# Feed-forward input transposed by VectorE and by way of DRAM in a fused attention and feed-forward kernel

## The chip, the cores and the metric

The kernel runs on one core of one Trainium2 chip. The time is device time of one execution in microseconds (us); lower is better. Everything is float32. Engines are named as in the profile: PE is TensorE, PEld its weight loads, DVE is VectorE, ACT is ScalarE, POOL is GpSimd, SP is SyncE, which here only issues DMAs.

## What is computed

One layer on 2048 tokens of width 256: a differential attention with 16 query and 8 key heads, then a gated feed-forward with Walsh-Hadamard transforms. Both are wrapped the same way: normalise, apply, normalise, add.

```python
x = x + _layernorm(_L0_attn_ref(_layernorm(x), ...))
x = x + _layernorm(_L0_ffn_ref(_layernorm(x), ...))

def _L0_ffn_ref(input, SU_ug, SU_dp, Wscale_ug, Wscale_dp, W_up, W_gate, W_down):
    x = fwht(x * SU_ug) / SCALE
    x_up = x @ W_up.T * (Wscale_ug[:INTER] * SCALE)
    x_gate = x @ W_gate.T * (Wscale_ug[INTER:] * SCALE)
    x = jax.nn.silu(x_gate) * x_up
    x = fwht(x * SU_dp) / SCALE
    return x @ W_down.T * (Wscale_dp * SCALE)
```

HIDDEN is 256 and INTER is 1024. The transforms are linear and are folded into the weights on the chip beforehand, so that per token the feed-forward is two products (gate and up, 256 to 1024), an elementwise step and one product (down, 1024 to 256).

## The kernel before

**Attention** is cut into 96 units of query rows, 24 for each of 4 groups of heads. Each unit goes through stages one step apart: `scores` on PE, the running minimum on DVE (L276, L287), `exponentials` on ACT, `combine` on DVE, then `turn`, which transposes 32x32 blocks on DVE (L353) and writes them to DRAM, `arrive`, which reads them back turned, `values` on PE (L377), `inverse` on POOL, `turn_out` and `arrive_out` (the same way by DRAM for the output, L421, L423, L433), `project_out` on PE (L442) and `accumulate` on DVE into `acc`, which holds the attention output of all tokens.

**Feed-forward** goes over blocks b of 256 tokens from b = 7 down to 0 (NS is 8), since the last group of heads finishes the late rows first. Partition p of a block holds two tokens, t = 0 and 1. The functions of a block:

- `load_x(b)`: POOL issues two DMAs of the residual x into `xr` (two buffers).
- `front1(b)`: statistics of the attention output (DVE, then a power on POOL, L93).
- `front2(b)`: normalises it (L97), adds x (L641), statistics of the sum.
- `front3(b)`: normalises the sum into `xr` (L97).
- `turn_ffn(b)`: four PE transposes of 128x128 into PSUM (`tx`, L653), one ACT copy into `fxnT` (L655), which holds features on partitions and the 256 tokens in columns, t = 0 in the first 128.
- `hidden(b, k)`, k = 0 to 3: 16 matmuls for gate and up (L666) into one PSUM tile; for each of its two chunks of 128 hidden features a sigmoid on ACT (L679) and two products on DVE (L680, L681) into `hT` (ten buffers).
- `back(b)`: 32 matmuls (L696) of `hT` with the down weights into `pd`.
- `finish1(b)`, `finish2(b)`: statistics of `pd`, normalisation, the sum with `acc`, and two DMAs of the result (L715).

PSUM tiles of the scores, of the hidden pieces, of `tx` and of `pd` share three buffers of one tag (`sc`). The two DVE transposes of `turn_out` write into one buffer (`xo`), which is free again when its DMA to DRAM (a tile of tag `do`, four buffers) has landed.

**Order.** The order of every engine's instructions is the order of the calls. The generator `ffn_pieces` yields the feed-forward in pieces. The list at the end of the kernel places the pieces into the attention's steps: block 7's hidden pieces in the last four steps with new units, then two pieces per step (before the step's own work and between), and all that is left after the last step. `last` is the number of units; `put(before, last - 5, turn_ffn, NS - 1)` places a call ahead of the work of step `last - 5`. Block 7's `load_x` and `front1` to `front3` stand near step `last - 11`. For the others the generator sets the order: after hidden(b, 0) come `front2(b-1)` and back(b+1), then finish(b+1) and hidden(b, 1), then `front3(b-1)` and hidden(b, 2), then `turn_ffn(b-1)`, `front1(b-2)` and hidden(b, 3), then hidden(b-1, 0).

Of the kernel before, what the change touches and what calls it, by code (L numbers as in the profile page):

```python
# [10 lines left out]
F32 = mybir.dt.float32  # L11
# [5 lines left out]
P = 128  # L17
# [11 lines left out]
NS = S // 256  # L29
# [19 lines left out]
def kernel(  # L49
# [14 lines left out]
    nc = tc.nc  # L64
# [3 lines left out]
    ident = const.tile([P, P], F32, name="ident")  # L68
# [14 lines left out]
    def rstd_of(pool, src, n, tag):  # L83

        st = pool.tile([P, 4, 6], F32, tag="st" + tag, name="st" + tag)
        mv = pool.tile([P, 4, 2], F32, tag="mv" + tag, name="mv" + tag)
        for t in range(n):
            nc.vector.bn_stats(st[:, t, :], src[t] if isinstance(src, list) else src[:, t, :])
            nc.vector.bn_aggr(mv[:, t, :], st[:, t, :])
        ve = pool.tile([P, 4], F32, tag="ve" + tag, name="ve" + tag)  # L90
        nc.vector.tensor_scalar(ve[:, :n], mv[:, :n, 1], EPS, None, ALU.add)
        rstd = pool.tile([P, 4], F32, tag="rs" + tag, name="rs" + tag)
        nc.gpsimd.tensor_tensor(rstd[:, :n], ve[:, :n], mhalf[:, :n], ALU.pow)  # L93
        return mv, rstd

    def normalise(dst, src, mv, rstd, t):
        nc.vector.tensor_scalar(  # L97
            dst, src, mv[:, t, 0:1], rstd[:, t : t + 1], ALU.subtract, ALU.mult
        )
# [7 lines left out]
    with ExitStack() as actx:  # L107
        ep = actx.enter_context(tc.tile_pool(name="ep", bufs=3))
        op = actx.enter_context(tc.tile_pool(name="op", bufs=2))
# [3 lines left out]
        dram = actx.enter_context(tc.tile_pool(name="dram", bufs=4, space=bass.MemoryType.DRAM))  # L113
        ps_s = actx.enter_context(tc.tile_pool(name="ps_s", bufs=3, space=PSUM))
# [11 lines left out]
        xnT = xtp.tile([P, 2, S], F32, name="xnT")  # L126
# [418 lines left out]
        ffn = {}  # L545
# [82 lines left out]
        def load_x(b):  # L628
            ffn["xr", b] = ffn["p"].tile([P, 2, HID], F32, tag="xr", name=f"xr_{b}", bufs=2)
            for s in range(2):  # L630
                nc.gpsimd.dma_start(ffn["xr", b][s::2], x2[b, s])


        def front1(b):
            ffn["ln", b] = rstd_of(ffn["p"], acc[:, ts(b, 2), :], 2, "a")

        def front2(b):
            y = acc[:, ts(b, 2), :]
            for t in range(2):
                normalise(y[:, t, :], y[:, t, :], *ffn["ln", b], t)  # L640
            nc.vector.tensor_add(y, ffn["xr", b], y)  # L641
            ffn["ln", b] = rstd_of(ffn["p"], y, 2, "b")

        def front3(b):
            for t in range(2):
                normalise(ffn["xr", b][:, t, :], acc[:, 2 * b + t, :], *ffn["ln", b], t)

        def turn_ffn(b):
            xr = ffn["xr", b]
            tx = ps_s.tile([P, 1024], F32, tag="sc", name=f"tx_{b}")[:, :512]  # L650
            for c in range(2):
                for t in range(2):
                    nc.tensor.transpose(tx[:, ts(2 * c + t, P)], xr[:, t, ts(c, P)], ident)  # L653
            xnT = ffn["p"].tile([P, 2, 256], F32, tag="fxnT", name=f"fxnT_{b}", bufs=2)
            nc.scalar.copy(xnT.rearrange("p c q -> p (c q)"), tx)  # L655
            ffn["xnT", b] = xnT

        def hidden(b, k):

            ps = ps_s.tile([P, 1024], F32, tag="sc", name=f"gu_{b}_{k}")  # L660
            xnT = ffn["xnT", b]
            for j in range(2):
                fc = 2 * k + j
                for n, which in enumerate(("gate", "up")):
                    for c in range(2):
                        nc.tensor.matmul(  # L666
                            ps[:, ts(2 * j + n, 256)],
                            lhsT=ffn[which][:, c, ts(fc, P)],
                            rhs=xnT[:, c, :],
                            start=(c == 0),  # L670
                            stop=(c == 1),
                        )
            for j in range(2):
                fc = 2 * k + j
                pg, pu = ps[:, ts(2 * j, 256)], ps[:, ts(2 * j + 1, 256)]
                wsu = colv[:, C_WSUG + fc : C_WSUG + fc + 1]
                wsg = colv[:, C_WSUG + NFC + fc : C_WSUG + NFC + fc + 1]
                hT = ffn["p"].tile([P, 256], F32, tag="hT", name=f"hT_{b}_{fc}", bufs=10)
                nc.scalar.activation(hT, pg, AF.Sigmoid, scale=wsg)  # L679
                nc.vector.scalar_tensor_tensor(hT, pg, wsg, hT, ALU.mult, ALU.mult)  # L680
                nc.vector.scalar_tensor_tensor(hT, pu, wsu, hT, ALU.mult, ALU.mult)  # L681
                ffn["hT", b, fc] = hT

        def back(b):

            if b:
                pd = ps_s.tile([P, 2, 512], F32, tag="sc", name=f"pd_{b}")
                pd = [pd[:, t, :HID] for t in range(2)]
            else:
                pd = [  # L690
                    ps_s.tile([P, 1024], F32, tag="sc", name=f"pd_{b}_{t}")[:, :HID]
                    for t in range(2)
                ]
            for t in range(2):
                for fc in range(NFC):
                    nc.tensor.matmul(  # L696
                        pd[t],
                        lhsT=ffn["hT", b, fc][:, ts(t, P)],
                        rhs=ffn["down"][:, fc, :],
                        start=(fc == 0),  # L700
                        stop=(fc == NFC - 1),
                    )
            ffn["pd", b] = pd

        def finish1(b, lo=0, n=2):
            ffn["ln", b, lo] = rstd_of(ffn["p"], ffn["pd", b][lo : lo + n], n, "c")

        def finish2(b, lo=0, n=2):
            tag, bufs = ("xr", 2) if lo else ("y", 1)
            z = ffn["p"].tile([P, 2, HID], F32, tag=tag, name=f"y_{b}_{lo}", bufs=bufs)[:, :n, :]  # L710
            for t in range(n):
                normalise(z[:, t, :], ffn["pd", b][lo + t], *ffn["ln", b, lo], t)
            nc.vector.tensor_add(z, z, acc[:, 2 * b + lo : 2 * b + lo + n, :])
            for s, engine in enumerate((nc.sync, nc.sync if b else nc.scalar)):
                engine.dma_start(outv[b, s][:, lo : lo + n, :], z[s::2])  # L715

        def ffn_pieces():
            for b in range(NS - 1, -1, -1):
                prev, nxt = b + 1 < NS, b > 0
                if nxt:  # L720
                    load_x(b - 1)
                yield hidden(b, 0)
                if nxt:
                    front2(b - 1)
                if prev:
                    yield back(b + 1)
                    finish1(b + 1)
                    finish2(b + 1)
                yield hidden(b, 1)
                if nxt:  # L730
                    front3(b - 1)
                yield hidden(b, 2)
                if nxt:
                    turn_ffn(b - 1)
                    if b > 1:
                        front1(b - 2)
                yield hidden(b, 3)
            back(0)
            for lo in range(2):
                finish1(0, lo, 1)  # L740
                finish2(0, lo, 1)

        pieces = ffn_pieces()

        def ffn_piece():
# [12 lines left out]
        before, mid, between, after = {}, {}, {}, {}  # L758

        def put(where, step, f, *args, **kw):  # L760
            where.setdefault(step, []).append(lambda: f(*args, **kw))
# [63 lines left out]
        last = len(units)  # L825
# [20 lines left out]
        begun = first + 13  # L846
        put(after, begun, open_ffn)
        put(after, begun, load_x, NS - 1)
        for j, part in enumerate((front1, front2, front3)):
            put(after, begun + j, part, NS - 1)  # L850
        put(after, begun + 2, front1, NS - 2)
        put(before, last - 5, turn_ffn, NS - 1)
        for where, step, count in (
            *((between, last - 4 + j, 1) for j in range(4)),
            *((w, last + j, 1) for j in range(LAG + 3) for w in (before, between)),
# [98 lines left out]
```

## Time and profile before

| | us |
|---|---|
| median of 3 runs (1462.11 to 1464.83) | 1464.06 |
| the profiled execution | 1462.91 |
| span of the profiled execution | 1461.1 |
| L653, PE transposes of `xr`, 32 instructions, busy | 5.9 |
| L655, ACT copies of `tx`, 8 instructions, busy | 4.6 |
| L666, PE matmuls of the hidden pieces, 512 instructions, busy | 131.5 |
| L696, PE matmuls of back, 256 instructions, busy | 56.8 |
| L421, DVE transposes of `turn_out`, 128 instructions, busy | 48.9 |

The granted clock of TensorE is 0.999 over the span. Busy time by stage:

```profile
1200.00:1250.00 50.00, 48.65 (x198) 37.09 (x197) 39.59 (x112) 23.96 (x59) 7.96 (x21) 1.00 0.89 185
1250.00:1300.00 50.00, 49.29 (x231) 42.90 (x231) 34.20 (x117) 27.68 (x69) 13.16 (x28) 1.00 0.39 102
...
1380.00:1400.00 20.00, 20.00 (x95) 17.66 (x95) 13.59 (x36) 3.98 (x9) 3.29 (x5) 1.00 0.06 19
```

The columns are the stretch and its length, then busy time with the number of instructions for PE, PEld, DVE, ACT and POOL, the granted clock, the share of DMA time and GB/s. Block 7's feed-forward begins at 1236 us; the last attention matmul (L442) ends near 1351 us; from there to the end only feed-forward blocks run. In a group of pipelined matmuls the length shown for one is longer than the distance to the next; the distance between the starts of two groups is what a group costs. A bracket behind an instruction holds the idle time ahead of it and the engine and line that ended it.

### The profile page before, as it was taken

Reading aid. Unit: us, or ns where it says so; the run is one execution under the profiler, and the core shown is the slowest. Engines: PE = TensorE matmul, PEld = TensorE weight load, DVE = VectorE, ACT = ScalarE, POOL = GpSimd, SP = SyncE. Lnnn points to the kernel's source line nnn. Section 1 sums busy time; section 2 is a strip of 40 time slices with the busy share of each in tenths; the row PEclk is TensorE's granted clock in tenths of the full one; section 3 lists DMA queues with packets and bytes.
Section 4 is the critical chain, followed back from the end, with each engine's and each line's share of the span. In section 5 each row is a group of like instructions: output and inputs, shape, how many; then the busy total and the mean of one; then the engine's idle time right before and its main releaser. Section 6 shows DMA issues by size and latency. Waiting matters only on the chain.

```text
span 1461.1 us, 17617 instructions
## 1 busy us (share of the span) xinstructions
PE 1441.2 (99%) x5484; PEld 1040.1 (71%) x5484; DVE 1038.5 (71%) x2412; ACT 516.9 (35%) x1125; POOL 359.1 (25%) x683
## 2 busy tenths in 40 slices
PE   8999999999999999999999999999999999999998
PEld 7567767756766777675677776675777767888887
DVE  5588888847666889644968779536877898756674
ACT  2453333323133334333333344333333444631211
POOL 2026735542007851011111111111111111121110
PEclk9999999999999999999999999999999999999999
DMA  3169889856487888831798888621999998522000
GB/s 116 33 162 195 185 194 220 167 103 132 91 194 147 164 190 198 170 80 51 155 184 177 172 202 169 141 65 52 194 209 189 196 183 181 131 79 58 30 22 15
DMA packets 494828, 204.50 MB, mean 140 GB/s; under 512 B 391088, under 2 KB 491952, under 8 KB 494736
## 3 DMA queue, kind: packets, MB, share of 16 engines
q1 hardware_dynamic: 491120, 194.17, 63.3%
q0 software_dynamic: 2480, 8.26, 2.1%
q8 instruction: 45, 0.74, 0.2%
q10 hardware_dynamic: 1136, 0.95, 0.2%
q14 instruction: 47, 0.39, 0.1%
HBM read 107.90 MB, written 95.42 MB: 139 GB/s over the span
## 4 chain that ended last, share of the span: by engine, by line
PE 92%; DVE 6%; issue 1%; ACT 1%; DMA 1%; SPq 0%; POOL 0%; POOLq 0%; DVEq 0%; ACTq 0%
PE po L377 30%; PE sc L261 29%; PE pp L173 11%; PE pout L442 7%; PE gu L666 7%; PE pv L202 4%; PE pd L696 4%; DVE e L276 1%; DVE e L334 1%; DVE e L353 1%; DMA wq<-in_wqkvT 1%; DVE e L287 0%; PE tx L653 0%; DVE xo L421 0%; DVE cf L329 0%
## 5 line engine op out<-in xcount | busy, mean ns | idle before, releaser
L261 PE MATMUL sc<-k,q 128*128 128x512 f32 (+7 forms) x1280 | 478.6, 520 | 8.7 <-DVE last L287 3.7
L377 PE MATMUL po<-v,pt 128*128 128x256 f32 x2176 | 485.4, 379 | 0.0
L377 PEld LDWEIGHTS po<-v,pt 128*128 128x128 f32 x2176 | 425.9, 196 | 57.1 <-issue 9.5
L261 PEld LDWEIGHTS sc<-k,q 128*128 128x128 f32 x1280 | 236.7, 190 | 229.3 <-issue 184.3
L302 ACT ACTIVATE e<-e,last 128x192 f32<-128x192 f32 (+28 forms) x256 | 299.6, 1171 | 217.9 <-DVE last L287 205.3
L276 DVE TENSOR_SCALAR_CACHE_REDUCE e<-sc 128x1024 f32<-128x1024 f32 (+15 forms) x248 | 231.1, 932 | 188.6 <-PE sc L261 187.8
L402 POOL TENSOR_TENSOR u<-ss,ed 128x1 f32<-128x1 f32 (+1 forms) x96 | 18.3, 191 | 764.7 <-ACT po L391 764.5
L388 ACT COPY osb<-po 128x256 f32<-128x256 f32 (+1 forms) x96 | 42.5, 443 | 457.5 <-PE po L377 450.1
L353 DVE STREAM_TRANSPOSE e<-e 128x768 f32<-128x768 f32 (+7 forms) x192 | 172.3, 937 | 6.7
L334 DVE SCALAR_TENSOR_TENSOR e<-e,cf,e 128x64 f32<-128x64 f32 (+31 forms) x128 | 173.8, 1378 | 3.4
L173 PE MATMUL pp<-xnT,wq 128*128 128x512 f32 (+1 forms) x408 | 170.8, 568 | 2.8 <-DMA wq<-in_wqkvT 2.6
L173 PEld LDWEIGHTS pp<-xnT,wq 128*128 128x128 f32 x408 | 76.7, 190 | 81.1 <-issue 74.6
L442 PE MATMUL pout<-wo,oT 128*128 128x256 f32 x512 | 120.9, 379 | 0.0
L276 DVE TENSOR_SCALAR_CACHE_REDUCE e<-sc,mx 128x320 f32<-128x320 f32 (+13 forms) x128 | 97.1, 759 | 21.3 <-PE sc L261 7.8
L442 PEld LDWEIGHTS pout<-wo,oT 128*128 128x128 f32 x512 | 97.3, 190 | 12.8
L679 ACT ACTIVATE hT<-gu,colv 128x256 f32<-128x256 f32 x64 | 30.3, 473 | 132.6 <-PE gu L666 91.1
L287 DVE CUSTOM_DVE_ANT_0 e<-sc,mask,mx 128x64 f32<-128x64 f32 x248 | 70.4, 284 | 8.9
L666 PE MATMUL gu<-fxnT,wgate 128*128 128x256 f32 x256 | 65.8, 379 | 0.2 <-DVE last L287 0.2
L666 PE MATMUL gu<-fxnT,wup 128*128 128x256 f32 x256 | 65.7, 379 | 0.0
L405 POOL TENSOR_SCALAR osb<-osb,f 128x256 f32<-128x256 f32 x128 | 61.3, 479 | 12.3
L403 POOL TENSOR_TENSOR f<-u,mhalf 128x1 f32<-128x1 f32 (+1 forms) x96 | 60.0, 625 | 7.5
L680 DVE SCALAR_TENSOR_TENSOR hT<-gu,colv,hT 128x256 f32<-128x256 f32 x64 | 30.9, 482 | 41.7 <-ACT hT L679 41.5
(102 smaller groups left out, 1112.6 us busy)
## 6 DMA issues: line engine op xcount, KB each, us to landing
dr<-e SPq DMA_DIRECT2D x20, 1024.0 KB, 4.7
pt<-dr SPq DMA_DIRECT2D x80, 256.0 KB, 5.9
dr<-e SPq DMA_DIRECT2D x20, 896.0 KB, 4.4
pt<-dr SPq DMA_DIRECT2D x80, 224.0 KB, 5.1
do<-xo SPq DMA_DIRECT2D x64, 256.0 KB, 3.8
oT<-do SPq DMA_DIRECT2D x256, 64.0 KB, 2.6
dr<-e SPq DMA_DIRECT2D x20, 768.0 KB, 4.3
pt<-dr SPq DMA_DIRECT2D x80, 192.0 KB, 4.4
```

The source lines that it names most:

```text
L173: nc.tensor.matmul(pp[:, 512 * h : 512 * h + n], lhsT=wq[:, c, ts(j, P)], rhs=xnT[:, c, cols4], start=(c == 0), stop=(c == 1),)
L261: nc.tensor.matmul(sc[:, 512 * k : 512 * k + ww], lhsT=qT[m][:, u.i, u.subs[a]].rearrange("d p q -> d (p q)"), rhs=kT[m][:, at + lo : at + ...
L276: nc.vector.tensor_scalar(dst, src, 1.0, best, ALU.mult, ALU.min, accum_out=u.mx[:, k0, c : c + 1],)
L287: nc.vector.tensor_tensor_reduce(e[:, L - 64 : L], sc[:, tail : tail + 64], mask, 1.0, best, ALU.add, ALU.min, accum_out=u.last[:, k0 : k0 ...
L302: nc.scalar.activation(e, e, AF.Exp, bias=u.last[:, 2 * a + m : 2 * a + m + 1], scale=-1.0, accum_out=u.d[:, a, m : m + 1],)
L334: nc.vector.scalar_tensor_tensor(e0, e1, cf[:, a : a + 1], e0, ALU.mult, ALU.add)
L353: nc.vector.transpose(xv[:, r], ev[:, r])
L377: nc.tensor.matmul(u.po[:, ts(a, HID)], lhsT=ptv[:, g, r, :], rhs=vt[:, kc, :], start=(kc == 0), stop=(kc == u.i),)
L403: nc.gpsimd.tensor_tensor(f[:, : u.ns], w[:, : u.ns], mhalf[:, : u.ns], ALU.pow)
L405: nc.gpsimd.tensor_scalar(u.osb[:, a, :], u.osb[:, a, :], f[:, a : a + 1], 16.0, ALU.mult, ALU.mult)
L442: nc.tensor.matmul(u.pout[:, :HID], lhsT=u.oT[:, c, p, :], rhs=wos[u.g][:, p, c, :], start=(p == 0 and c == 0), stop=(p == 1 and c == 1),)
L666: nc.tensor.matmul(ps[:, ts(2 * j + n, 256)], lhsT=ffn[which][:, c, ts(fc, P)], rhs=xnT[:, c, :], start=(c == 0), stop=(c == 1),)
```

## The change

The four PE transposes, the PSUM tile `tx` and the ACT copy are taken out. `turn_ffn` now does what `turn_out` does: two DVE transposes of 32x32 blocks into the shared buffer `xo`, and one DMA on SP to a DRAM tile of the tag `do`. A new function `arrive_ffn` reads the block back with four DMAs on SP, one for each 32 partitions of `fxnT`, in rows of 64 elements. Token columns of `fxnT` now alternate between t = 0 and t = 1, so `back` reads its weights from `hT` with a step of two. In the generator `front3(b-1)`, `turn_ffn(b-1)` and `arrive_ffn(b-1)` stand right behind back(b+1) and ahead of finish(b+1), and `front1(b-2)` stays ahead of hidden(b, 3). Block 6 is taken out of the generator and is loaded, normalised and turned by calls placed in the attention's steps, as block 7 is; block 7's turn moves from step `last - 5` to `last - 7`, its reads to `last - 6`.

```diff
--- before.py
+++ after.py
@@ -646,13 +646,26 @@
                 normalise(ffn["xr", b][:, t, :], acc[:, 2 * b + t, :], *ffn["ln", b], t)
 
         def turn_ffn(b):
-            xr = ffn["xr", b]
-            tx = ps_s.tile([P, 1024], F32, tag="sc", name=f"tx_{b}")[:, :512]
-            for c in range(2):
-                for t in range(2):
-                    nc.tensor.transpose(tx[:, ts(2 * c + t, P)], xr[:, t, ts(c, P)], ident)
+
+            xo = op.tile([P, 512], F32, tag="xo", name=f"xf_{b}", bufs=1)
+            xv = xo.rearrange("p (g a c r) -> p r g a c", a=4, g=2, r=2)
+            ev = ffn["xr", b].rearrange("p r (g a c) -> p r g a c", g=2, a=4)
+            for r in range(2):
+                nc.vector.transpose(xv[:, r], ev[:, r])
+            dr = dram.tile([2, 4, 32, 4, 64], F32, tag="do", name=f"df_{b}")
+            nc.sync.dma_start(
+                dr.rearrange("g b q a w -> (b q) g (a w)"),
+                xo.rearrange("p (g w) -> p g w", g=2),
+            )
+            ffn["dx", b] = dr
+
+        def arrive_ffn(b):
             xnT = ffn["p"].tile([P, 2, 256], F32, tag="fxnT", name=f"fxnT_{b}", bufs=2)
-            nc.scalar.copy(xnT.rearrange("p c q -> p (c q)"), tx)
+            for a in range(4):
+                nc.sync.dma_start(
+                    xnT[ts(a, 32)].rearrange("e c (b w) -> e (c b) w", w=64),
+                    ffn["dx", b][:, :, :, a, :].rearrange("g b q w -> q (g b) w"),
+                )
             ffn["xnT", b] = xnT
 
         def hidden(b, k):
@@ -695,7 +708,7 @@
                 for fc in range(NFC):
                     nc.tensor.matmul(
                         pd[t],
-                        lhsT=ffn["hT", b, fc][:, ts(t, P)],
+                        lhsT=ffn["hT", b, fc][:, t::2],
                         rhs=ffn["down"][:, fc, :],
                         start=(fc == 0),
                         stop=(fc == NFC - 1),
@@ -717,23 +730,24 @@
         def ffn_pieces():
             for b in range(NS - 1, -1, -1):
                 prev, nxt = b + 1 < NS, b > 0
-                if nxt:
+                if nxt and prev:
                     load_x(b - 1)
                 yield hidden(b, 0)
-                if nxt:
+                if nxt and prev:
                     front2(b - 1)
                 if prev:
                     yield back(b + 1)
+                if nxt and prev:
+                    front3(b - 1)
+                    turn_ffn(b - 1)
+                    arrive_ffn(b - 1)
+                if prev:
                     finish1(b + 1)
                     finish2(b + 1)
                 yield hidden(b, 1)
-                if nxt:
-                    front3(b - 1)
                 yield hidden(b, 2)
-                if nxt:
-                    turn_ffn(b - 1)
-                    if b > 1:
-                        front1(b - 2)
+                if b > 1:
+                    front1(b - 2)
                 yield hidden(b, 3)
             back(0)
             for lo in range(2):
@@ -848,8 +862,14 @@
         put(after, begun, load_x, NS - 1)
         for j, part in enumerate((front1, front2, front3)):
             put(after, begun + j, part, NS - 1)
+        put(after, begun + 2, load_x, NS - 2)
         put(after, begun + 2, front1, NS - 2)
-        put(before, last - 5, turn_ffn, NS - 1)
+        put(before, last - 7, turn_ffn, NS - 1)
+        put(before, last - 6, arrive_ffn, NS - 1)
+        put(after, last - 5, front2, NS - 2)
+        put(after, last - 4, front3, NS - 2)
+        put(before, last - 3, turn_ffn, NS - 2)
+        put(before, last - 2, arrive_ffn, NS - 2)
         for where, step, count in (
             *((between, last - 4 + j, 1) for j in range(4)),
             *((w, last + j, 1) for j in range(LAG + 3) for w in (before, between)),
```

## The prediction

> **What bounds the kernel now.** I read the busy totals first, then the chain of waits, then tables by stage of the last 260 us, where the feed-forward blocks run, and last the order of time on TensorE, VectorE and the DMA queue there.
>
> ```profile
> PE 1441.2 (99%) x5484; PEld 1040.1 (71%) x5484; DVE 1038.5 (71%) x2412; ACT 516.9 (35%) x1125; POOL 359.1 (25%) x683
> ...
> PE 92%; DVE 6%; issue 1%; ACT 1%; DMA 1%; SPq 0%; POOL 0%; POOLq 0%; DVEq 0%; ACTq 0%
> ```
>
> The first line is busy time by engine, the second the shares of the chain that ended last. TensorE (PE) is busy for 99% of the span and holds 92% of the chain: work taken off PE counts in full unless another engine then falls behind. VectorE (DVE) is next with 6%, so it is the one to watch, and the change gives it work.
>
> What the transposes cost is read from PE's order of time (start, length, instructions). First in the last 100 us, where only feed-forward runs, then in the stretch shared with attention:
>
> ```profile
> 1378.65 1.03 PE L666 MATMUL gu<-fxnT,wup 128*128 128x256 f32 x4
> 1379.69 0.87 PE L653 MATMUL tx<-ident,xr 128*128 128x128 f32 x4
> 1380.40 1.03 PE L666 MATMUL gu<-fxnT,wgate 128*128 128x256 f32 x4
> ```
>
> ```profile
> 1305.89 1.89 PE L442 MATMUL pout<-wo,oT 128*128 128x256 f32 x8
> 1307.61 0.60 PE L653 MATMUL tx<-ident,xr 128*128 128x128 f32 x4
> 1308.05 1.03 PE L666 MATMUL gu<-fxnT,wgate 128*128 128x256 f32 x4
> ```
>
> Groups of four hidden matmuls start 0.865 us apart (1380.40, 1381.27, 1382.13). Across the transposes of block 2 the step is 1380.40 - 1378.65 = 1.75, so they cost 0.885: 0.44 of streaming and 0.44 of waiting for DVE's normalisation (L97), which ends only at 1379.96. In the shared stretch the same four cost 1308.05 - 1307.61 = 0.44.
>
> **What is removed.** Block 7 (1219.57): nothing, since PE then waits 1.27 us for DVE anyway before its next scores at 1221.44. Blocks 6, 5 and 4 (1273.04, 1307.61, 1333.09): 3 x 0.44 = 1.32. Block 3: from 1357.70, when its forerunner's four end, to 1358.79: 1.09. Blocks 2, 1, 0: 0.885 + 0.885 + 0.895 = 2.67. Together **5.1 us** of PE. The eight copies on ScalarE (L655, 0.57 each) go too; ScalarE is 35% busy and off the chain, so they count as nothing.
>
> **What is moved.** Block 6 is normalised two steps earlier. Now its front2 stands in DVE's order at 1255.32 to 1258.05, ahead of the activation products and score reductions that PE needs:
>
> ```profile
> 1258.46 1.89 PE L442 MATMUL pout<-wo,oT 128*128 128x256 f32 x8
> 1260.65 0.59 PE L261 MATMUL sc<-k,q 128*128 128x192 f32 x2 [0.30 <-DVE hT L681]
> 1261.48 0.56 PE L261 MATMUL sc<-k,q 128*128 128x192 f32 x2 [0.23 <-DVE last L287]
> 1262.22 1.10 PE L666 MATMUL gu<-fxnT,wgate 128*128 128x256 f32 x4 [0.18 <-DVE last L287]
> ```
>
> Eight output matmuls take 1.73, so PE is free at 1260.19; the four score matmuls of 192 columns need 0.65 (0.216 for 256); the next group starts at 1262.22: 1.38 us lost to DVE. With 2.7 us of DVE work gone from in front, that loss should go. Its new places are DVE idle times: front2 after the step that ends on DVE at 1231.0 (idle 4.65 until 1235.69), front3 and the two block transposes after 1246.2 (idle 1.99; they take 0.69 + 0.76). The transposes share one buffer (xo) with attention's, whose next one, at 1249.55, must now wait for block 6's write, issued about 1247.8 and landed by 1250 to 1252 (2.2 to 3.8 us); DVE idles there until 1252.18 today, so some 0.3 us, covered by the 2.7 set free. Block 7's transposes fall into 1200.4 to 1200.9 (idle 0.56): 0.76 + 0.04 less 0.56 is 0.25 late, and the next idle 0.72 before 1212.12 takes that up; I charge **0.3** as the bound. Gain here: 1.4 - 0.3 = **1.1**.
>
> **What is added in the tail.** Two block transposes per block on DVE, and a round trip by way of DRAM. Attention's own pair, same shapes and queue, gives both prices:
>
> ```profile
> 1336.59 0.76 DVE L421 STREAM_TRANSPOSE xo<-osb 128x256 f32<-128x256 f32 x2
> ```
>
> ```profile
> 1337.38 0.38 SPq L423 DMA_DIRECT2D do<-xo  x1
> 1339.58 1.79 SPq L433 DMA_DIRECT2D oT<-do  x4
> ```
>
> The second fence is SyncE's queue: the write is issued, 2.20 us later the four reads start, their issue takes 1.79, and reads land 2.0 after issue (median after 1290). So from the transposes' end to the data: 0.05 + 2.2 + 1.8 + 2.0 = about 6.1.
>
> [...]
>
> Now DVE's round in one block, from starts in its order of time:
>
> ```profile
> 1388.02 0.48 DVE L680 SCALAR_TENSOR_TENSOR hT<-gu,colv,hT 128x256 f32<-128x256 f32 x1 [0.91 <-ACT hT L679]
> ...
> 1390.48 0.73 DVE L97 TENSOR_SCALAR acc<-acc,mva,rsa 128x256 f32<-128x256 f32 x2
> ...
> 1393.18 0.17 DVE L91 TENSOR_SCALAR veb<-mvb 128x2 f32<-128x2 f32 x1
> 1394.42 0.43 DVE L88 BATCH_NORM_STATS2 stc<-pd 128x6 f32<-128x256 f32 x1 [1.07 <-PE pd L696]
> ...
> 1396.68 1.00 DVE L97 TENSOR_SCALAR y<-pd,mvc,rsc 128x256 f32<-128x256 f32 x2 [0.87 <-POOL rsc L93]
> ...
> 1398.38 0.48 DVE L680 SCALAR_TENSOR_TENSOR hT<-gu,colv,hT 128x256 f32<-128x256 f32 x1
> ```
>
> The products of one hidden piece take 2.47 (1398.38 to the next work at 1400.85, with one wait of 0.54 for ScalarE inside). front2 takes 2.70 up to L91 at 1393.18; from such an L91 through GpSimd's power to the first user is 1.05 (1395.63 to 1396.68), so 3.75 to front3. front3 is 0.75, the transposes 0.80, finish1 and finish2 3.96 (1394.42 to 1398.38), front1 1.38. One round: 4 x 2.47 + 3.75 + 0.75 + 0.80 + 3.96 + 1.38 = **20.52 us**. PE's round without transposes is 96 matmuls of 0.216 = **20.73**, against 21.61 now (1383.86 to 1405.47). DVE fits by 0.2. Front3 now waits for GpSimd (0.8 idle) where other work stood; finish, the hidden products and the output writes queue behind it, about 1.4 us later, and PE does not feel it: the accumulator of back is freed 2 us before its buffer is needed again, and the last products reach back about 0.8 before they are used.
>
> Counted from the start of hidden(b,0): products from 4.17 to 6.63, front3 at 10.38, transposes end 11.93, data at 11.93 + 6.1 = 18.0, needed at 20.73. 2.7 us to spare. On SyncE the outputs stand behind the reads, which end at 15.9, when they are ready anyway. POOL's loads of x keep their place behind front1's power.
>
> The weights of back are now read with a step of two elements. Attention's value matmuls already do so (L377), and 32 of them take 6.91 in the chain, as 32 of back (L696) do: no cost.
>
> **The sum.** 5.1 + 1.1 = 6.2 us. The profiled execution took 1462.91 (span 1461.1), so 1456.7; the median of the runs shown, 1464.06, is 1.15 higher, which gives 1457.9. I forecast **1458.0**.
>
> **Rivals.**
> 1. *VectorE sets the pace in the tail.* For: only 0.2 us between the two rounds, and PE already waits for DVE at each tail transpose. Against: every idle time counted is still in the sum. The new buffer wait, a second 0.54 wait of DVE for ScalarE before hidden(b,2), and later GpSimd answers could add 0.5 to 1.5. At 22.0 per round PE loses 4 x 1.3 less the 0.8 to spare = 4.4: **1462.4**; at 21.3 it loses 1.5: 1459.5.
> 2. *The round trip comes late, and the kernel is slower.* Mechanism: hidden(b-1,0) waits for fxnT on PE in each of the last four blocks. It decides once the trip exceeds 20.73 - 11.93 = 8.8 us, and the whole is slower once it exceeds 8.8 by over 1.5 per block. Over the whole run such writes take up to 6.5 and such reads up to 5.4 us: 6.5 + 1.8 + 5.4 = 13.7, 4.9 late, four times 19.6: **1477**. For: 256-byte pieces, two transfers in a row, one queue. Against: those maxima come from stretches with DMA 90% busy; the tail has 4 to 8%. With the run's medians (3.8 + 1.8 + 2.6 = 8.2) it still fits. A milder form, 2.2 late each time, gives 1467.
> 3. *Nothing shows.* The transposes were cover for DVE's lateness and PE waits as long at the next instruction that needs DVE: then only the 1.3 of the shared stretch and part of the 1.1 stay: **1462.5**. Against: hidden(b,3) needs nothing from DVE that is late.
>
> [...]
>
> **Chances.** Forecast 0.60, rival 1 0.14 (half of it still over 0.2% faster), rival 2 0.18, rival 3 0.08. What a measurement can tell from no change is 0.2%, 2.9 us: faster means under 1461.1, slower over 1467.0. Faster 0.60 + 0.07 = 0.67; same 0.07 + 0.08 and 0.01 of rival 2's mild form = 0.16; slower 0.17. Range: low end with all of 6.5 gained on the fastest run shown (1462.1): 1455.6; high end the two no-change cases with 0.6 to spare: 1463.0. Without the slower case, the likeliest one's own range is 1455.6 to 1460.
>
> **What would show it.** Hidden groups 0.865 apart with no hole across the block change and rounds of 20.73 in the tail; the 1.38 us at the score matmuls of 192 columns gone; DVE busy some 77% in the tail with a small wait for PE left per round; fxnT landed 2 to 3 us before use. I would be wrong if PE waits at hidden(b,0) for a DMA, or at back for the products, or if DVE's order after 1246 delays attention's combination.

## The result and the profile after

The changed kernel takes 1457.06 us (median of 5 runs, 1454.12 to 1458.70) against 1464.06: a ratio of 0.9951 (0.9939 to 0.9962), 7.0 us between the medians. Its profiled execution took 1457.06 as well (span 1455.3). The forecast was 1458.0.

Busy totals and the chain of waits of the kernel after:

```profile
PE 1437.0 (99%) x5452; PEld 1040.1 (71%) x5452; DVE 1043.5 (72%) x2428; ACT 513.8 (35%) x1117; POOL 360.8 (25%) x683
...
PE 94%; DVE 5%; DMA 1%; issue 1%; ACT 0%; SPq 0%; POOLq 0%; DVEq 0%
```

PE has 32 instructions less, the eight times four transposes; DVE has 16 more. PE's share of the chain rises by 2 points and DVE's falls by one: some of the waiting for DVE is gone too.

The totals don't say where. For that I cut PE's order of time at five starts that every version has: the first value matmul (L377), the first hidden matmul (L679 now), and the first matmuls of back(7), back(5) and back(0) (L709 now). Between them lie section I (attention, with block 7's transposes near its end), II (with block 6's), III (with those of blocks 5 and 4) and IV (those of 3, 2, 1 and 0; five rounds of the tail). Each number is a difference of two starts, in us:

| kernel | start to first L377 | I | II | III | IV | I to IV |
|---|---|---|---|---|---|---|
| before | 67.94 | 1168.30 | 49.79 | 56.13 | 105.66 | 1379.88 |
| after | 69.83 | 1167.07 | 47.94 | 55.25 | 101.87 | 1372.13 |
| gained | -1.89 | 1.23 | 1.85 | 0.88 | 3.79 | 7.75 |

The four sections gain 7.75. The first 70 us, which the change doesn't touch, took 1.9 longer in the one execution profiled: the profiles differ by 5.85, the medians by 7.0. That start-up is taken up below.

The tail in the order of time on PE (start, length, instructions), at the change from block 3 to block 2, where the kernel before had its transposes:

```profile
1378.94 1.03 PE L679 MATMUL gu<-fxnT,wup 128*128 128x256 f32 x4
1379.80 1.03 PE L679 MATMUL gu<-fxnT,wgate 128*128 128x256 f32 x4
```

The last group of block 3 and the first of block 2 are 0.86 apart, as all groups of four here are, without a hole; the rounds are 20.72 long, 96 x 0.216. The hole at the score matmuls of 192 columns is closed too, in the same view of the shared stretch:

```profile
1260.84 0.81 PE L261 MATMUL sc<-k,q 128*128 128x192 f32 x4
1261.49 1.03 PE L679 MATMUL gu<-fxnT,wgate 128*128 128x256 f32 x4
```

Before, 0.65 of work and 1.38 of waiting lay between the output matmuls and the next hidden group; now the four score matmuls run as one group, 1261.49 - 1260.84 = 0.65.

What DVE and SyncE's queue do in the tail, one block (idle time ahead of an instruction and what ended it stand in the bracket):

```profile
1383.96 0.48 DVE L693 SCALAR_TENSOR_TENSOR hT<-gu,colv,hT 128x256 f32<-128x256 f32 x1 [0.62 <-ACT hT L692]
...
1390.78 0.77 DVE L654 STREAM_TRANSPOSE xf<-xr 128x256 f32<-128x256 f32 x2
```

```profile
1391.58 0.38 SPq L656 DMA_DIRECT2D df<-xf  x1
1393.78 1.80 SPq L665 DMA_DIRECT2D fxnT<-df  x4
1395.68 1.26 SPq L728 DMA_DIRECT2D out<-y  x2
```

The transposes end at 1391.5, the write is issued at once, the reads 2.20 later, the last of them at 1395.1; the reads of this block land 2.1 to 2.3 after issue, so the data is there at about 1397.3. PE needs it at 1400.52, some 3.2 later. The 0.62 at L693 is the one place of the round where DVE waits because PE isn't further on: the bracket names ScalarE, and ScalarE's instruction waits 1.15 for PE's hidden matmuls there (its start is 1383.45).

### The profile page after: what moved, and what is told of

The parts are those of the page before. It is cut to its first block, busy times and chain, and to the rows that moved or that the text cites. A ratio compares the mean times of both kernels' runs of the same rounds, so it can differ in the third digit from the quotient of the medians.

```text
span 1455.3 us, 17627 instructions
## 1 busy us (share of the span) xinstructions
PE 1437.0 (99%) x5452; PEld 1040.1 (71%) x5452; DVE 1043.5 (72%) x2428; ACT 513.8 (35%) x1117; POOL 360.8 (25%) x683
## 4 chain that ended last, share of the span: by engine, by line
PE 94%; DVE 5%; DMA 1%; issue 1%; ACT 0%; SPq 0%; POOLq 0%; DVEq 0%
PE po L377 30%; PE sc L261 29%; PE pp L173 12%; PE gu L679 8%; PE pout L442 8%; PE pv L202 4%; PE pd L709 4%; DVE e L276 1%; DVE e L334 1%; DVE e L353 1%; DMA wq<-in_wqkvT 1%; DVE xo L421 0%; DVE e L287 0%; DVE cf L329 0%; PE pst L506 0%
## 5 line engine op out<-in xcount | busy, mean ns | idle before, releaser
L377 PE MATMUL po<-v,pt 128*128 128x256 f32 x2176 | 485.4, 379 | 0.0
L377 PEld LDWEIGHTS po<-v,pt 128*128 128x128 f32 x2176 | 425.9, 196 | 57.0 <-issue 9.5
L692 ACT ACTIVATE hT<-gu,colv 128x256 f32<-128x256 f32 x64 | 30.3, 474 | 128.6 <-PE gu L679 83.1
L679 PE MATMUL gu<-fxnT,wgate 128*128 128x256 f32 x256 | 65.8, 379 | 0.0
L679 PE MATMUL gu<-fxnT,wup 128*128 128x256 f32 x256 | 65.7, 379 | 0.0
L202 PE MATMUL pv<-wq,xnT 128*128 128x256 f32 x256 | 57.4, 379 | 0.0
```

The source lines that it names most:

```text
L202: nc.tensor.matmul(pp[:, ts(t, 256)], lhsT=xnT[:, c, ts(nb * 4 + t, P)], rhs=wq[:, c, 768:1024], start=(c == 0), stop=(c == 1),)
L377: nc.tensor.matmul(u.po[:, ts(a, HID)], lhsT=ptv[:, g, r, :], rhs=vt[:, kc, :], start=(kc == 0), stop=(kc == u.i),)
L679: nc.tensor.matmul(ps[:, ts(2 * j + n, 256)], lhsT=ffn[which][:, c, ts(fc, P)], rhs=xnT[:, c, :], start=(c == 0), stop=(c == 1),)
```

## The experiments

Each edit is against the kernel after. Sections are read from one profile per kernel. They repeat to 0.1 us (section I to 0.3), while whole times of one kernel scatter by 1 to 5 us. Between the profiles nearly all of that lies in the start-up.

**Order alone, and the way by DRAM alone.** The change does two things: it moves the turn forward by one piece and more, and it takes the turn off PE. The first kernel keeps the new order and transposes on PE; the second keeps the way by DRAM for blocks 6 to 0 and puts it where PE's transposes stood before.

```diff
+        def turn_pe(b, pool=None, tag="sc"):
+            xr = ffn["xr", b]
+            tx = (pool or ps_s).tile([P, 1024 if tag == "sc" else 512], F32, tag=tag, name=f"tx_{b}")[:, :512]
...
+                    nc.tensor.transpose(tx[:, ts(2 * c + t, P)], xr[:, t, ts(c, P)], ident)
...
+            nc.scalar.copy(xnT.rearrange("p c q -> p (c q)"), tx)
...
                     front3(b - 1)
-                    turn_ffn(b - 1)
-                    arrive_ffn(b - 1)
...
                 yield hidden(b, 2)
+                if nxt and prev:
+                    turn_pe(b - 1)
```

> The new order alone, with the transposes on PE again. Four sections of PE's time, each between two starts: I first value matmul (L377) to first hidden matmul, II to back(7), III to back(5), IV to back(0). Before 1168.30, 49.79, 56.13, 105.66; after 1167.07, 47.94, 55.25, 101.87. Theory: normalising ahead alone removes the 1.38 us hole of section II and the wait for L97 in section IV, and nothing else: I 1168.3, II 48.4, III 56.1, IV 103.6 (four times 0.44 of transposes left), together 3.5 us less than before and 4.3 more than after. Rival 'the order is the whole gain': all four as after, 7.7 less than before. Rival 'the order gives nothing': all four as before.

Measured: 1462.59 (10 runs, 1461.22 to 1463.29), ratio 0.9981 (0.9971 to 0.9991). Sections 1168.33, 48.33, 56.13 and 104.00, together 3.1 less than before: II has lost its hole, IV has lost most of the waits for normalisation (it was expected at 103.6; in the round of block 3 the transposes still cost 0.8), I is as before. From block 2 on the rounds are 21.15, and in them the transposes cost 0.43 and no wait:

```profile
1402.08 0.60 PE L676 MATMUL tx<-ident,xr 128*128 128x128 f32 x4
1402.51 1.03 PE L689 MATMUL gu<-fxnT,wgate 128*128 128x256 f32 x4
```

The order is worth 3.1, and taking the transposes off PE 4.7 more: two fifths of the gain need no VectorE transposes at all. Of the 4.7, 1.26 lie in section I. They are the price of a PSUM buffer, and a transpose on PE with another buffer saves them too (under "Why section I gained"). That leaves about 3.4 for which VectorE and DRAM are needed, an estimate, since the new order and the other buffer weren't run together for all blocks.

The second kernel, with block 6 back in the generator:

```diff
                     yield back(b + 1)
-                if nxt and prev:
-                    front3(b - 1)
-                    turn_ffn(b - 1)
-                    arrive_ffn(b - 1)
...
                 yield hidden(b, 1)
+                if nxt:
+                    front3(b - 1)
                 yield hidden(b, 2)
+                if nxt:
+                    turn_ffn(b - 1)
+                    arrive_ffn(b - 1)
...
                 yield hidden(b, 3)
```

> VectorE's transposes and the way by DRAM for blocks 6 to 0, but in the old order (front3 behind finish, the transposes ahead of hidden(b,3)); block 7 as after. Theory: the round trip is no longer covered. In the tail DVE turns a block only behind the products of hidden(b,2), about 21.2 us after hidden(b,0) starts, and the data come 6.1 later, at 27.3 instead of 20.73: PE waits about 6.6 us in each of the last four or five blocks. Section IV 128 to 135 instead of 101.87, section III 56 to 68, I as after; the time 1485 to 1505. Rival 'the place in the order does not matter, it is the engine': all sections as after, time 1457.

Measured: 1520.33; sections 1167.00, 58.78, 72.43 and 139.20, together 57.5 more than before, and tail rounds of 30.2 to 30.3. III, IV and the time lie above what was expected: PE waits for the reads in all seven blocks and not in four or five, and PE loses time behind the waits too. One block:

```profile
1443.22 1.03 PE L679 MATMUL gu<-fxnT,wup 128*128 128x256 f32 x4
1450.94 2.05 PE L679 MATMUL gu<-fxnT,wgate 128*128 128x256 f32 x4 [6.69 <-DMA fxnT<-df]
1452.78 1.91 PE L679 MATMUL gu<-fxnT,wup 128*128 128x256 f32 x4
```

A wait of 6.6 was expected, 6.7 came, but the round is 9.5 longer than 20.72. The other 2.8 or so stand behind the wait: the next groups start at 1452.78, 1454.48 and 1456.19, 1.7 to 1.84 apart instead of 0.865. The table of stages over the same stretch shows a lower granted clock there (stretch, length, busy time of PE, PEld, DVE, ACT and POOL with instructions, granted clock, DMA share, GB/s):

```profile
1451.00:1453.00 2.00, 2.00 (x5) 1.64 (x6) 0.00 (x0) 0.00 (x0) 0.00 (x0) 0.50 0.00 0
...
1455.00:1457.00 2.00, 2.00 (x8) 1.65 (x7) 0.00 (x0) 0.00 (x0) 0.00 (x0) 0.68 0.00 0
1457.00:1459.00 2.00, 2.00 (x11) 1.83 (x10) 0.97 (x2) 0.62 (x2) 0.00 (x0) 1.00 0.00 0
```

Behind this pause the granted clock reads 0.50 up to 1455, 0.68 from 1455 to 1457 and 1.00 from there. The four groups up to back at 1457.11 take 6.17 instead of 4 x 0.865 = 3.46: with these 2.7 the wait of 6.69 is paid 1.4 times. At two other pauses of this kernel, 4.01 us before 1322.28 and 8.91 before 1359.88, the three groups behind take 4.35 and 4.76 instead of 2.60, so 1.8 and 2.2 come on top: 1.4 and 1.2 times. So the way by DRAM without the new order costs 57 us, the order without it gains 3, and both together gain 7.7.

**Why section I gained.** I had block 7's transposes down as free, and its two on DVE as a loss of 0.3; the section gained 1.23. One explanation is the PSUM tile `tx`: it takes one of the three buffers that the scores use, until ScalarE has copied it. Two kernels with the new order and blocks 6 to 0 as after put block 7's turn back on PE: once in the scores' tag, once in the tag of attention's value products.

```diff
-        put(before, last - 7, turn_ffn, NS - 1)
-        put(before, last - 6, arrive_ffn, NS - 1)
+        put(before, last - 5, turn_pe, NS - 1)
...
+        put(before, last - 5, turn_pe, NS - 1, ps_o, "o")
```

The last line is the second kernel's, in place of the third.

> Only block 7 is transposed by PE as before, into the PSUM tag that the scores use; all else as after. Section I lost 1.23 us by the change, where I had charged 0.3 more. Theory: tx took one of the three PSUM buffers that the scores rotate through, and held it until ScalarE had copied it, so that PE waited 1.27 us. Then section I is 1168.3 again (1.2 more than after) and sections II to IV are as after (47.9, 55.25, 101.9). Rival 'it was the DVE order or ScalarE's queue': section I 1167.1 to 1167.5.

> As e3_block7_pe_sc, the same order on every engine, but tx in the PSUM tag of the value and output matmuls (o). Theory (the buffer): the scores find their buffer free, section I is 1167.1 to 1167.6, at most the 0.44 of the transposes more than after. Rival 'the four matmuls and the copy themselves': section I 1168.3 as in e3_block7_pe_sc.

Measured: section I 1168.34 and 1167.04; all others as after (47.94, 55.25, 101.87 or 101.88 in both). Whole times 1458.11 and 1458.44: the second lost 1.7 in the start-up. PE's order of time, first with `tx` in the scores' tag, then in the other:

```profile
1221.28 0.60 PE L676 MATMUL tx<-ident,xr 128*128 128x128 f32 x4
1223.15 4.17 PE L261 MATMUL sc<-k,q 128*128 128x256 f32 x13 [1.27 <-DVE last L287]
```

```profile
1222.92 0.60 PE L676 MATMUL tx<-ident,xr 128*128 128x128 f32 x4
1223.36 1.14 PE L261 MATMUL sc<-k,q 128*128 128x256 f32 x4
1224.80 3.43 PE L261 MATMUL sc<-k,q 128*128 128x256 f32 x11 [0.30 <-DVE last L287]
```

With a buffer of its own the transposes let four score matmuls through at once and only 0.30 of waiting stays; with one of the scores' the same four wait 1.27 for DVE to free the next. The kernel after waits here too:

```profile
1223.38 3.54 PE L261 MATMUL sc<-k,q 128*128 128x256 f32 x12 [0.74 <-DVE last L287]
```

That is 0.74, or 0.44 more than 0.30, because the transposes that filled the gap are gone. So the matmuls themselves were free, as predicted; the buffer cost 1.3. And I of the kernel after is 1167.07 with block 7's transposes on DVE, 1167.04 without: they cost nothing that can be seen. The three profiles with `tx` in the scores' tag have I at 1168.30 to 1168.34, the eleven others at 1167.00 to 1167.27.

**How near DVE is to its limit.** One and three extra pairs of block transposes per block go into a scratch tile, in the last four blocks, right behind the real pair.

```diff
             ffn["dx", b] = dr
+            if b < 4:
+                for k in range(3):
+                    xx = op.tile([P, 2, HID], F32, tag="osb", name=f"xx_{b}_{k}")
...
+                    for r in range(2):
+                        nc.vector.transpose(xxv[:, r], ev[:, r])
```

> One more pair of block transposes on VectorE, of the same data into a buffer that nobody reads, behind each block's own pair, blocks 3 to 0. In the trace of after, DVE waits 0.61 us for PE in each tail round, and a pair takes 0.69 of its round. Theory (DVE has little to spare and PE does not feel it yet): overshoot 0.1 per round, taken up by the 0.8 that the last products reach back early: section IV 101.9 to 102.3. Rival 1 'DVE sets the pace already': 0.7 more per round, section IV 104.5.

> Three more pairs per block instead of one: 2.1 us more per round, 1.5 over what DVE has free. Theory: DVE sets the pace, four rounds of 22.2, less the 0.8 to spare once: section IV 106 to 108. Rival 'DVE is far from the bound': 101.9. If it is DVE's pace, PE waits at back (L709) for the products or at hidden for a PSUM buffer, never for a DMA.

Measured: with one pair 1456.45 and IV 101.87, unchanged; with three 1461.74 and IV 105.82, rounds of 21.9 to 22.0. IV is just under the 106 to 108 expected. PE waits in three blocks, 0.9 to 1.0 each in its own order of time, at one of the two places that the expectation had named:

```profile
1400.34 1.13 PE L685 MATMUL gu<-fxnT,wgate 128*128 128x256 f32 x4 [0.98 <-DVE y L97]
```

The group ahead started at 1398.33, so this one should have at 1399.20. It waits for L97, DVE's read of `pd` in finish2, to free a PSUM buffer, and not at back for products in `hT`. A pair takes 0.69 from start to next start: between 0.7 and 2.1 us more of DVE work per block, VectorE becomes the bound. In these rounds none of DVE's waits goes back to PE any more; those left are for ScalarE and GpSimd, which wait for DVE.

**How much time the trip has to spare.** The turn moved behind finish of the block before.

```diff
                     front3(b - 1)
-                    turn_ffn(b - 1)
-                    arrive_ffn(b - 1)
                 if prev:
                     finish1(b + 1)
                     finish2(b + 1)
+                if nxt and prev:
+                    turn_ffn(b - 1)
+                    arrive_ffn(b - 1)
```

> turn_ffn and arrive_ffn stand behind finish1 and finish2 instead of ahead of them; nothing is added or taken away. The transposes end 3.9 us later. Theory: the data had 3.0 us to spare in the tail, so hidden(b-1,0) waits 0.9 to 1.2 us on PE in each of the last four rounds: section IV 105 to 107, and the idle time ahead of hidden's first matmul is put down to a DMA. Rival 'the round trip has far more to spare' or 'DVE's round is what counts': section IV 101.9.

Measured: 1466.30; IV 109.01, 7.1 more than after and more than the expectation allowed; rounds of 22.3 to 22.4. The late turn on DVE accounts for a part. The rest is on SyncE's queue; its order of time in one block, and PE's behind it:

```profile
1422.66 1.26 SPq L728 DMA_DIRECT2D out<-y  x2
1424.02 0.54 SPq L656 DMA_DIRECT2D df<-xf  x1
1426.40 1.79 SPq L665 DMA_DIRECT2D fxnT<-df  x4
```

```profile
1429.84 1.10 PE L679 MATMUL gu<-fxnT,wgate 128*128 128x256 f32 x4 [1.34 <-DMA fxnT<-df]
```

Two output DMAs now stand ahead of the write and take 1.26 us to issue; in the kernel after they stand behind the reads. The write goes out 0.8 us after the transposes end (1423.2), not at once, and the reads 2.38 after it, not 2.20: 1.0 of the 3.2 us to spare goes to the order on one queue. With the 3.9 that the turn comes later, that makes 1.7 too late; in this block the group starts 1.5 late (1429.84 against 1428.34). PE waits in all four blocks, 1.3 to 2.1. In two the bracket names the DMA, as here; in two it names DVE's L693, of a piece whose PSUM buffer this group doesn't take, so I put those down to the data as well, which wasn't tried. Behind three of these pauses the granted clock reads 1.00; behind the fourth, shown here, the next groups start 0.94, 0.86 and 0.87 apart, as they do behind the others to 0.01.

**The shared buffer.** Block 6's transposes hold `xo`, and attention's next transpose waits. In DVE's order of time of the kernel after:

```profile
1253.07 0.77 DVE L421 STREAM_TRANSPOSE xo<-osb 128x256 f32<-128x256 f32 x2 [2.78 <-DMA df<-xf]
```

That is 2.78 where I had allowed 0.3. Blocks 7 and 6 get a buffer of their own:

```diff
-            xo = op.tile([P, 512], F32, tag="xo", name=f"xf_{b}", bufs=1)
+            if b > 5:
+                xo = ffn["p"].tile([P, 2, HID], F32, tag="y", name=f"xf_{b}", bufs=1)
+                xo = xo.rearrange("p s w -> p (s w)")
+            else:
+                xo = op.tile([P, 512], F32, tag="xo", name=f"xf_{b}", bufs=1)
```

> Blocks 7 and 6 turn into a buffer of their own (the one of the result, idle until block 7's finish) instead of the one shared with attention. In the trace of after, DVE waits 2.78 us at 1250 for block 6's write before it may turn attention's output. Theory: that wait goes and nothing else changes, since PE has no hole there: sections as after within 0.1 (II 47.94). Rival 'the shared buffer costs time': section II shorter by 0.3 to 1.5.

Measured: 1456.63, sections 1167.04, 47.94, 55.25, 101.87. The wait goes and nothing is gained: DVE then stands 1.86 at the next instruction, which needs ScalarE.

**The same for attention's input.** The last 512 tokens of attention's input are also transposed on PE. Two kernels turn them on VectorE and by way of DRAM, with the projection that uses them moved back; in the second the transposes stand behind the score reductions, and the projection moves one step further. The second's edit:

```diff
-        put(after, 1, turn_in, 3)
+        put(after, 1, turn_last)
+        put(after, 1, arrive_last)
...
-        put(mid, 2, project_heads, 0, 3, 0, both=True)
...
+        put(before, 3, project_heads, 0, 3, 0, both=True)
```

> A try at going further: after, and the last 512 tokens of the attention's input, transposed by PE at the start (eight matmuls, 0.87 us, behind 0.40 idle), go by VectorE and DRAM too; the tokens are loaded two to a partition row, and the projection of the first queries of that block moves behind the scores of step 2. From the start of PE's transposes of tokens 1024 to 1535 (L506) to the first value matmul it is 37.36 us after and 37.38 before. Theory: 36.1 (1.27 less), all later sections as after, the time 1455.8 against 1457.06. Rival 'the data come late': written about 53.5, eight reads on each of two queues, there at 60.5, wanted at about 62; if the trip takes 3 us longer, PE waits and the stretch is 37 to 40.

> e9_input_block3 again, with three things changed: VectorE's four transposes stand behind the score reductions of step 1 instead of ahead of them, the reads are eight on SyncE, and the projection of the block's first queries moves on to the start of step 3. In e9_input_block3 the data came in time, but PE stood 1.53 us at the values' projection (L202) because the reductions, and with them a PSUM buffer, came 1.4 us later. Theory: that wait goes, the stretch from PE's transposes of tokens 1024 to 1535 to the first value matmul is 36.1 to 36.6 instead of 37.36 (after) and 37.99 (e9_input_block3), all later sections as after, 0.8 to 1.3 us in all. Rival 'DVE has no room there either': it stays at 37.4 or more, with PE's wait at another instruction.

Measured, from PE's transposes of tokens 1024 to 1535 to the first value matmul: 37.99 and 36.91, against 37.36; 36.1, and then 36.1 to 36.6, had been expected. The first one lost where it should have gained; the data came in time, but the four transposes (1.42 us) stood ahead of the score reductions on DVE, and PE waited for a PSUM buffer:

```profile
50.09 3.69 PE L202 MATMUL pv<-wq,xnT 128*128 128x256 f32 x16 [1.53 <-DVE last L287]
```

The second gained 0.45 there (a wait of 0.45 is left at the same place), and its section I is 0.1 longer, which is within the 0.3 to which that section repeats. Whole times: 1456.85 (4 runs, 1454.45 to 1458.51; ratio 0.9947, 0.9930 to 0.9964) and 1458.05 (5 runs, 1457.00 to 1458.21; ratio 0.9955, 0.9941 to 0.9968): neither differs measurably from the kernel after.

**The start-up.** The time to the first value matmul ranges from 67.2 to 71.4 over these profiles, in code that most of the edits leave alone. All of them have ten matmuls on the identity (`warm`), the first input transposes, and then a pause in which PE waits, mostly for the first weights. The last kernel fills the pause with these ten calls once more, to see whether the clock is behind the spread; the kernel after ran again beside it on the same chip.

```diff
+        def keep_warm():
...
+            for k in range(WARM):
+                nc.tensor.matmul(warm[:, :P], lhsT=ident, rhs=ident, start=True, stop=True)
...
         put(before, 0, turn_first, 0)
+        put(before, 0, keep_warm)
         put(before, 0, norm_first, 1)
```

> After, and ten more matmuls on the identity (as those at the start, their result unused) on PE between the first transposes of x and the first projection, where PE stands idle from 7 to about 9.6 us. In most profiles of this study the granted clock is 0.5 for 4 to 6 us behind that pause, in the others 1.0, which moves the start of the first value matmul between 67.2 and 71.4 us; in e2_dram_old_order it is 0.5 for 5 us behind each pause of 6.7 us in the tail, in e7_turn_after_finish it stays at 1.0 behind pauses of 1.4 us. Theory: the pause brings the low clock; with PE busy, the clock stays 1.0 in the first 20 us, the first value matmul starts at 67 to 68 us in each run, the median is 1454 to 1455 with a spread under 2 us. Rival 'the low clock at the start has nothing to do with the pause': still 0.5 at 10 to 14 us, median as after.

> The changed kernel as it is, beside e11_keep_warm on the same chip: 1456 to 1458, spread 3 to 5 us from the clock of the first 20 us.

Measured: with the pause filled 1455.26 (5 runs, 1454.84 to 1455.91; ratio to before 0.9942, 0.9930 to 0.9954), and the first value matmul at 67.68; the kernel after 1455.99 (6 runs, 1454.23 to 1459.10; ratio 0.9949, 0.9933 to 0.9964), and 68.83. The first median is just above the 1454 to 1455 expected of it, the second 0.01 below its range. The spread falls from 4.9 to 1.1 us; the medians are too near to call one faster. Tables of stages, the filled one first:

```profile
9.00:12.00 3.00, 3.00 (x18) 2.69 (x17) 0.72 (x2) 0.70 (x2) 2.66 (x6) 1.00 0.86 280
```

```profile
9.00:12.00 3.00, 3.00 (x8) 2.38 (x9) 0.49 (x2) 0.00 (x0) 2.71 (x6) 0.50 0.94 309
```

Same stretch, PE busy throughout in both; 18 instructions at a granted clock of 1.00, 8 at 0.50. What the other profiles and runs show of this stands in the last section.

## Why the prediction was right, point by point

- *What is removed, 5.1.* Blocks 6 to 0 came out as read: 0.44 in II, 0.88 in III, and 3.79 in IV against 1.09 + 2.67 = 3.76. The reading that each tail transpose costs 0.44 of streaming and 0.44 of waiting for L97 is shown by the kernel with the new order and PE's transposes: from block 2 on it drops the second part and keeps the first.
- *Block 7, "nothing".* This is the mis-sized term. The matmuls were free behind DVE's wait of 1.27, but that wait was itself made by the PSUM buffer they held: 1.3, shown by changing the tag alone. I had counted the time of the instructions and not the buffer they hold. The bound of 0.3 for its transposes on DVE wasn't needed either: the difference is 0.03, too small to be told from none. Together they put the sum 1.5 too low, 6.2 against 7.75.
- *Block 6's new places, 1.4.* Right: II gained 1.85, which is 1.38 and 0.44. The wait for `xo` was 2.78, not 0.3: the write was issued at 1248.53, behind attention's reads on SyncE, not at 1247.8, and landed 4.4 later, not 2.2 to 3.8. That nothing came of it is because DVE waits for ScalarE there anyway.
- *DVE's round, 20.52 against 20.73.* The sign is right, the size a little high: DVE waits 0.62 per round of 20.72 for PE, so its work is 20.1, and it is busy for 75% of the tail against the 77% forecast. Added work shows that the limit lies where this says: one pair more is free, three are not. Rival 1 had this limit as its mechanism; it would have needed 0.6 more than the round has.
- *The round trip.* It took 5.8 from the end of the transposes to the data, against 6.1, and 3.2 were to spare against 2.7. The forecast added the landing to the end of the last read's issue; it counts from that issue's start (1395.1 to 1397.3). In this block the write landed 2.1 after its issue, the reads 2.2 (median). Rival 2 is a real mechanism, seen twice: PE waits 1.3 to 2.1 per block where the turn stands behind finish, and the round is 9.5 longer where it stands where it used to. What keeps it off is the order alone.
- *Rival 3*, that PE waits as long at the next instruction that needs DVE, falls: no hole in the tail.
- *The engine of the transposes.* With the order held the same, transposing on TensorE is 4.7 us slower here, 1.3 of it for the PSUM buffer. With the old order, where nothing covers the longer way, it would have been the better choice: there VectorE and DRAM lost 57 us.

The median came 0.9 below the forecast. The gain was 1.5 larger than predicted; in the profiled execution a start-up 1.9 longer hid that, and the medians show 0.7 less than the sections. So the terms of the tail and of block 6 were right as argued, but that the time came so near is in part luck: block 7's missing 1.2 and the start-up, which the forecast took as unchanged, pull in opposite directions.

## What to carry to other kernels

When TensorE is the bound, count for each transpose on it the streaming, the wait for its input and the PSUM buffer it holds until the copy: here 0.44, 0.44 and once 1.3 us. The way by VectorE and DRAM cost nothing here because it starts early enough (6 us, and 3 to spare), and an order that lets it start early is worth having even without it. Look at what stands ahead of the write on its DMA queue (two output DMAs took 1.26 us to issue), and at how much VectorE has left per round (0.7 us more was free, 2.1 was not), before putting more there.

## What was not expected of the hardware

A pause of TensorE cost 1.8 to 2.7 us more than its length in one kernel and 0.1 more in another. In the kernel with the way by DRAM in the old order PE waits for the reads seven times, 46.0 us in all, the longest time 8.9. Around the pause of 6.69 that ends at 1450.94 the granted clock reads 1.00 from 1444 to 1449, 0.61 from 1449 to 1451, 0.50 from 1451 to 1455, 0.68 from 1455 to 1457 and 1.00 behind that. If it was either 0.50 or 1.00 within each of these stretches, it was low from 1449.4 to 1456.3, an estimate from these readings: it fell some 5 us into the pause and stayed low for 5 us of work behind it. Behind the pauses of 4.01, 8.91 and 6.69 us PE loses 1.8, 2.2 and 2.7 us more. Behind three pauses of 1.34 to 2.07 us in the tail (the turn behind finish) the clock reads 1.00, and the first three groups take 2.66 to 2.67 instead of 2.60.

The start has a low clock as well in ten of the 14 profiles, and its length, estimated in the same way from tables of stages, sorts them by the time to the first value matmul:

| low clock in the first 20 us | profiles | first value matmul, us |
|---|---|---|
| none | 4: before, the way by DRAM in the old order, the first of the two input kernels, the pause filled | 67.24 to 67.94 |
| 3.4 to 3.5 us | 5: after (twice), block 7 with `tx` in the scores' tag, one extra pair, the own buffer | 68.83 to 69.83 |
| 6.8 to 6.9 us | 5: the new order on PE, block 7 with `tx` in the other tag, three extra pairs, the turn behind finish, the second input kernel | 70.54 to 71.39 |

In the ten with a low clock, the pause ahead of the first projection is a single one of 1.8 to 3.4 us. In the first row it is broken into pauses of at most 1.1 us in two and filled in one; only in the kernel before is it a single one, of 2.55. Length alone doesn't decide: block 7 with `tx` in the scores' tag has a pause of 2.55 too, and there the clock reads 0.53 from 10 to 12 us; and the second profile of the kernel after has one of 1.81, up to 8.83, and reads 0.89 from 7 to 9 and 0.50 from 9 to 12. What else decides, no run shows.

In the first profile of the kernel after the clock reads 0.98 over the first 100 us and 1.00 from 100 to 1200. For the runs without a profile the mean granted clock is on record. On the chip of the last two kernels, runs of the kernel before took 1461.7 to 1462.7 at 0.999, 1463.9 to 1464.0 at 0.998 and 1465.4 to 1466.0 at 0.997; the kernel after 1454.2 to 1454.5 at 0.999 and 1.000, 1455.6 to 1456.4 at 0.998 and 1458.4 to 1459.1 at 0.997; with the pause filled, all five are at 0.999 or 1.000. So the scatter of some 4 us goes with the mean granted clock, in both kernels, and at the same clock they are 7 to 8 us apart. That it is the start's clock in these runs too is an estimate from the profiles.
